# Layer 1 of the last two graphs in a two-layer graph kernel: gathered rows in one buffer, neighbour sums ordered ahead of the product with W, the graph's sum added on VectorE

## The chip, the cores and the metric

The kernel runs on one core of a Trainium2 chip. The metric is device time in microseconds of that core, the median of three runs. The kernel before takes 2736.29 us (2734.39 to 2737.78).

A core has five engines, each with its own queue of instructions: TensorE (PE, with its weight loads PEld), VectorE (DVE), ScalarE (ACT), GpSimd (POOL) and SyncE (SP). They wait for each other through semaphores. POOL issues the gathers and scatters (indirect DMAs); SP issues plain DMAs.

## What is computed

32 graphs share one adjacency matrix of 512 nodes; each node has 512 features, and about 1 in 128 entries of the matrix is 1, so a node has some four neighbours. Two layers follow each other, both with a residual:

```python
# layer 0: attention with 8 heads over the neighbours
h = relu(layernorm(x))
q, k, v = h @ Wq + bq, h @ Wk + bk, h @ Wv + bv
x = x + softmax(q k^T / 8 + (1 - adj) * -1e9) v @ Wo + bo
# layer 1: graph attention
h = relu(layernorm(x)) @ W
s1, s2 = h @ a1, h @ a2
e = leaky_relu(s1[i] + s2[j], 0.2) * adj
x = x + elu(softmax(e) h + beta * h)
```

In layer 1 the entries outside the adjacency are zero before the softmax, not minus infinity. So each row of the softmax is (sum over all nodes) plus a correction over the neighbours, with weight exp(e) - 1. The kernel therefore adds up the neighbours' rows with these weights, adds the graph's sum over all nodes, adds the node's own row times beta and the denominator, and only then multiplies by W, once.

## The kernel before, in words

**Tiles and stages.** A graph is cut into four tiles of 128 nodes. The edges of a tile are laid out as four groups of 128 edge slots. For each group one gather (an indirect DMA on POOL, L946) brings the neighbours' rows to the 128 partitions, and a matrix product with a 0/1 matrix (32 columns) sums the slots of each node into 32 rows of a PSUM tile. `stage_a` does norm, queries, keys and values of graph b; `stage_b` does the neighbour work of layer 0 for graph b and, LAG = 2 graphs behind, that of layer 1 for graph b - 2, out of the same gathered rows. After the last graph's layer 0 there is no layer 0 left to share with: for the last two graphs (30 and 31) `stage_b` runs with layer 1 alone and gathers 520-wide rows out of the tables `th0` and `th1`. A row holds the neighbour's s2 value at place 0 (HO) and its h row behind it.

**Layer 1 of one tile** (`edge_weights`, `layer1`), with the lines of the profile:

1. four gathers (L946), each 128 rows of 520 values, into two buffers of the ring `kv`, two rows to a buffer (a buffer holds 2 x 1552 values a partition, and there are five);
2. the edge weights: s1 + s2 (L1127, twice, one for each buffer), slope (L1131), exp on ACT (L1133), minus one and mask (L1134), spread over the 0/1 matrix into `wv` (L1140);
3. the neighbour sums on TensorE (L987, four instructions of the program, eight in the profile), and a product with one column for the denominators (L42, `pd<-one,wv`);
4. on DVE the denominators (L1162 to L1164) and the node's own row (L1170), for which ACT has made the relu of the norm (L756);
5. four transposes on TensorE (L737);
6. the graph's sum added while the transposed tile is moved from PSUM into `gT`: four ACT instructions, one for each 128 features, the sum as their bias (L1181);
7. the product with W on TensorE (L42, `pd<-w,gT`);
8. elu: two ACT instructions (L1190, L1191) and two on DVE (L1195, L1196), and a scatter of the tile to the output (L767 on POOL).

For the last two graphs the s1 values come by another way than for the others: they are transposed (L1100), copied by ACT (L1102), stored and read back by SP (L1103, L1108), and picked on DVE (L1112, L1113). The graph's sum comes from the column sums of h (L1081), copied by ACT (L1085), transposed and reduced (L1087).

**What sets the order.** All operations are given to a planner (`Plan`) with an engine, an estimated length, a due time (`key`) and the buffers that they read and write. The planner plays the program through with its estimates, gives out the buffers of each ring in the order of due times, and of the operations ready on an engine takes the one that is due first. What it writes out is a fixed order on every engine; the chip then runs that order with real waits. Due times count in steps of S = 20 for a tile: in layer 1, the sums at k = kb + S, the transposes and the graph's sum at k + 0.485 S, the product with W at k + 0.88 S, elu at k + 1.05 S and the store 0.15 S behind it; the edge weights at kb + 0.6 S.

Of the kernel before, what the change touches and what calls it, by code (L numbers as in the profile page):

```python
# [19 lines left out]
P = 128  # L20
# [19 lines left out]
def product(nc, out, lhsT, rhs, start=True, stop=True):  # L40

    nc.tensor.matmul(out, lhsT, rhs, start=start, stop=stop)  # L42
# [22 lines left out]
class Plan:  # L65
# [153 lines left out]
def kernel(  # L219
# [515 lines left out]
    def turned(p, src):  # L735
        for c in range(C):
            nc.tensor.transpose(p[:, ts(c, P)], src[:, ts(c, P)], ident)  # L737
# [196 lines left out]
    def stage_b(b):  # L934

        s = st[b] if b < B else None
        old = st[b - LAG] if b >= LAG else None
        if old is not None:
            old["dn"] = buf("dn", f"dn{b}")
        if s is not None:  # L940
            s["x1"], s["hx"] = [None] * T, [None] * T
            s["mv1"], s["s1"] = buf("mv1", f"mv1_{b}"), buf("s1", f"s1_{b}")
            s["rd"] = buf("rd", f"rd{b}")

        def gather(dst, tab, t, g):
            nc.gpsimd.indirect_dma_start(  # L946
                dst, None, tab.ap, bass.IndirectOffsetOnAxis(ap=idx[:, t, g : g + 1], axis=0),
                bounds_check=N + DUMMY - 1, oob_is_err=False,
            )

        for t in range(T):
            kb = base(T * b + t)
            slots = [buf("kv", f"kv{b}_{t}_{i}") for i in range(2)]
            held = [{n: buf(None, n) for n in ("K", "V", "H")} for _ in range(2)]
            of = {KO: "KVH", VO: "VH", HO: "H"}
            for g in range(NG):
                for tab, c0, c1 in st[b]["tab"]:
                    op("POOL", 1.3, kb - 0.85 * S + 0.1 * g, lambda sl=slots[g // 2], g=g, t=t, tab=tab, c0=c0, c1=c1: gather(
                        sl.ap[:, g % 2, c0:c1], tab, t, g),
                       r=[tab, C_["idx"]],  # L960
                       w=[(slots[g // 2], (g % 2, c0)), *((held[g // 2][n], (g % 2, "row")) for n in of[c0])],
                       dma=P * (c1 - c0) * 4)
            if s is not None:
                qs = [buf("qe", f"qe{b}_{t}_{i}") for i in range(2)]
                for q in qs:
                    q.q, q.s1 = buf(None, "q"), buf(None, "s1")
                for g in range(NG):
                    op("POOL", 1.3, kb - 0.84 * S + 0.1 * g, lambda q=qs[g // 2], g=g, t=t: nc.gpsimd.indirect_dma_start(  # L968
                        q.ap[:, g % 2, :], None, s["qtab"].ap,
                        bass.IndirectOffsetOnAxis(ap=qidx[:, t, g : g + 1], axis=0),  # L970
                        bounds_check=N, oob_is_err=False),
                       r=[s["qtab"], C_["qidx"]], w=[(x, g % 2) for x in (qs[g // 2], qs[g // 2].q, qs[g // 2].s1)],
                       dma=P * QW * 4)
            wvb = edge_weights(b - LAG, t, kb, slots, held, qs if s is not None else None) if old is not None else None
            pv = layer0(b, t, kb, slots, held, qs, old is not None) if s is not None else None
            if old is not None:
                layer1(b - LAG, t, kb, slots, held, wvb, pv)
                if t == T - 1:
                    op("DVE", 0.16, kb + 1.6 * S, lambda: nc.vector.tensor_tensor(
                        dmax, dmax, old["dn"].ap[:, 0:2, :], op=ALU.max), r=[old["dn"]], w=[C_["dmax"]])  # L980
        if s is not None:
            self_sums(b, base(T * b + 6))

    def edge_sums(out, lhs, slots, c0, n):

        for g in range(NG):
            nc.tensor.matmul(out(g), lhs(g), slots[g // 2].ap[:, g % 2, c0 : c0 + n], start=True, stop=True)  # L987
# [131 lines left out]
    def edge_weights(b, t, kb, slots, held, qs):  # L1119

        s = st[b]
        k1 = kb + 0.6 * S
        z, wvb = buf("z", f"z{b}_{t}"), buf("wv", f"wv{b}_{t}")
        for i in range(2):
            def add(i=i):
                s1 = s["s1e"].ap[:, t, 2 * i : 2 * i + 2] if qs is None else qs[i].ap[:, :, D]
                nc.vector.tensor_tensor(z.ap[:, 2 * i : 2 * i + 2], s1, slots[i].ap[:, :, HO], op=ALU.add)  # L1127
# [3 lines left out]
        op("DVE", 0.2, k1, lambda: nc.vector.scalar_tensor_tensor(  # L1131
            z.ap, z.ap, ALPHA, z.ap, op0=ALU.mult, op1=ALU.max), w=[z])
        op("ACT", 0.25, k1, lambda: nc.scalar.activation(z.ap, z.ap, AF.Exp), w=[z])  # L1133
        op("DVE", 0.2, k1, lambda: nc.vector.scalar_tensor_tensor(  # L1134
            z.ap, z.ap, -1.0, nzE[:, t, :], op0=ALU.add, op1=ALU.mult), r=[C_["nzE"]], w=[z])
        if b + LAG < B:
            for i in range(2):
                op("DVE", 0.1, k1, lambda i=i: nc.vector.tensor_copy(
                    slots[i].ap[:, :, HO], z.ap[:, 2 * i : 2 * i + 2]), r=[z, (slots[i], "use")], w=[(held[i]["H"], "z")])
        op("DVE", 0.35, k1, lambda: nc.vector.tensor_tensor(  # L1140
            wvb.ap.rearrange("p (g r) -> p g r", r=G), oh[:, ts(t, NG), :],
            z.ap.unsqueeze(2).to_broadcast([P, NG, G]), op=ALU.mult), r=[z, C_["OH"]], w=[wvb])
        return wvb

    def layer1(b, t, kb, slots, held, wvb, pv):
        s = st[b]
        px, g = buf("D", f"pg{b}_{t}"), buf("w", f"g{b}_{t}")
        o = op("PE", 1.02, kb + S, lambda: edge_sums(
            lambda i: px.ap[ts(i, G), :], lambda i: wvb.ap[:, ts(i, G)], slots, HO + 1, D),
               r=[*((x, "use") for x in slots), *((h["H"], "rows") for h in held), wvb], w=[px], form=4)  # L1150
        plan.reserve(o, g)
        k = kb + S
        x1, dn = s["x1"][t], s["dn"]
        op("ACT", 0.8, k, lambda: relu(g.ap, x1.ap, s["mv1"].ap, t), r=[x1, (s["mv1"], t)], w=[g])

        if pv is None:
            pd = buf("D", f"pn{b}_{t}")
            op("PE", 0.2, kb + S, lambda: product(nc, pd.ap[:, 0:1], wvb.ap, one32[:, 0:1]), r=[wvb], w=[pd])

        def den():  # L1160
            src, by = (pd.ap[:, 0:1], float(G)) if pv is None else (pv.ap[:, 1, 4 * VW : 4 * VW + 1], 1.0)
# [10 lines left out]
            )  # L1172

        op("DVE", 0.75, k, own, r=[px, (dn, t)], w=[g])
        pt, gT, py, y = buf("D", "pt"), buf("gT", f"gT{b}_{t}"), buf("D", "py"), buf("w", f"y{b}_{t}")
        oo = op("PE", 0.45, k + 0.485 * S, lambda: turned(pt.ap, g.ap), r=[g], w=[pt])
        plan.reserve(oo, gT)

        def add_all():
# [2 lines left out]
                    gT.ap[:, c, :], pt.ap[:, ts(c, P)], AF.Identity, bias=s["cs"].ap[:, c : c + 1]  # L1182
                )

        op("ACT", 1.5, k + 0.485 * S, add_all, r=[pt, s["cs"]], w=[gT])
        oo = op("PE", 3.43, k + 0.88 * S, lambda: dense(py.ap, gT.ap, w1), r=[gT, C_["w1"]], w=[py])
        plan.reserve(oo, y)

        def halves():
# [5 lines left out]
            nc.vector.scalar_tensor_tensor(y.ap, y.ap, 1.0, x1.ap, op0=ALU.min, op1=ALU.add)  # L1195
            nc.vector.tensor_tensor(y.ap, y.ap, py.ap, op=ALU.add)  # L1196
# [252 lines left out]
```

## Time and profile before

| | |
|---|---|
| median of three runs | 2736.29 us |
| the profiled execution's own time | 2723.47 us |
| its span | 2721.6 us |
| PE busy | 2648.3 us (97%) |
| DVE, ACT, POOL busy | 2049.9, 1934.4, 1831.2 us |
| DMA | 790 MB, 289 GB/s over the span |
| first product with W of graph 30 starts | 2649.42 us |
| last product with W of graph 31 starts | 2707.68 us |

The profile records one execution. The span runs from the first to the last instruction; times in it are counted from its start. A line of the timeline gives start, length, engine, line of the kernel, operation, output and input by the program's names (numbers of buffers left out), how many instructions are merged, and in brackets the engine's idle time before it and what ended that. `w` is a ring of row buffers, `pd` a ring of PSUM tiles; the matrix W has the program's name `w1`, shown as `w` in `pd<-w,gT`.

### The profile page before, as it was taken

Reading aid. Unit: us, or ns where it says so; the run is one execution under the profiler, and the core shown is the slowest. Engines: PE = TensorE matmul, PEld = TensorE weight load, DVE = VectorE, ACT = ScalarE, POOL = GpSimd, SP = SyncE. Lnnn points to the kernel's source line nnn. Section 1 sums busy time; section 2 is a strip of 40 time slices with the busy share of each in tenths; the row PEclk is TensorE's granted clock in tenths of the full one; section 3 lists DMA queues with packets and bytes.
Section 4 is the critical chain, followed back from the end, with each engine's and each line's share of the span. In section 5 each row is a group of like instructions: output and inputs, shape, how many; then the busy total and the mean of one; then the engine's idle time right before and its main releaser. Section 6 shows DMA issues by size and latency. Waiting matters only on the chain.

```text
span 2721.6 us, 39762 instructions
## 1 busy us (share of the span) xinstructions
PE 2648.3 (97%) x10220; PEld 1213.2 (45%) x10220; DVE 2049.9 (75%) x5200; ACT 1934.4 (71%) x6215; POOL 1831.2 (67%) x1710
## 2 busy tenths in 40 slices
PE   8999999999999999999999999999999999999886
PEld 4444444444444444444444444444444444444332
DVE  7768777777777777777777777777777777777663
ACT  1557777687877777777777777777777777777763
POOL 2776766666766766766766776676676676675763
PEclk9999999999999999999999999999999999999988
DMA  5988998888988988988988988988888888888863
GB/s 180 252 290 320 307 307 291 297 294 305 311 296 289 321 292 296 314 297 288 316 298 292 326 291 290 321 289 303 312 296 292 305 309 303 297 310 286 303 211 117
DMA packets 237457, 790.08 MB, mean 290 GB/s; under 512 B 34667, under 2 KB 34675, under 8 KB 237222
## 3 DMA queue, kind: packets, MB, share of 16 engines
q0 software_dynamic: 156736, 644.99, 70.3%
q1 hardware_dynamic: 80486, 142.48, 14.0%
q8 instruction: 83, 1.36, 0.2%
q14 instruction: 152, 1.25, 0.1%
HBM read 617.88 MB, written 169.46 MB: 289 GB/s over the span
## 4 chain that ended last, share of the span: by engine, by line
PE 88%; DMA 3%; issue 3%; DVE 2%; ACT 2%; POOL 2%; POOLq 0%; SPq 0%; DVEq 0%; ACTq 0%
PE pd L42 46%; PE pd L858 26%; PE pd L737 6%; PE pd L987 4%; PE px L987 4%; DMA qe<-qtab,qidx 1%; ACT kv L1014 1%; PE pd L918 1%; DMA kv<-tkv,idx 1%; PE pd L1081 1%; POOL kv L946 1%; POOL qe L968 0%; POOL x L762 0%; DMA x<-in_x_dram,perm 0%; DVE s L1003 0%
## 5 line engine op out<-in xcount | busy, mean ns | idle before, releaser
L1014 ACT ACTIVATE kv<-kv 128x64 f32<-128x64 f32 x4096 | 1011.8, 335 | 5.2
L968 POOL DMA_INDIRECT qe<-qtab,qidx x512 | 556.0, 1086 | 223.0 <-issue 114.0
L946 POOL DMA_INDIRECT kv<-tab,idx x480 | 508.2, 1059 | 164.6 <-issue 113.6
L42 PE MATMUL pd<-wo,oT 128*128 128x512 f32 x1032 | 468.6, 597 | 2.5 <-ACT oT L1051 2.4
L42 PE MATMUL pd<-w,gT 128*128 128x512 f32 x1024 | 466.1, 598 | 3.6 <-ACT gT L1181 3.6
L42 PE MATMUL pd<-wq,hT 128*128 128x512 f32 x1024 | 465.0, 597 | 2.2 <-ACT hT L782 2.2
L762 POOL DMA_INDIRECT x<-in_x_dram,perm x252 | 359.5, 1426 | 85.1 <-issue 50.3
L1000 DVE TENSOR_TENSOR qe<-qe,kv 128x1024 f32<-128x1024 f32 x256 | 312.1, 1220 | 44.4 <-DMA qe<-qtab,qidx 35.6
L1003 DVE TENSOR_REDUCE s<-qe 128x16 f32<-128x1024 f32 x256 | 310.5, 1214 | 0.1
L42 PEld LDWEIGHTS pd<-w,gT 128*128 128x128 f32 x1024 | 195.7, 192 | 249.5 <-issue 234.0
L42 PEld LDWEIGHTS pd<-wo,oT 128*128 128x128 f32 x1032 | 196.3, 192 | 245.0 <-issue 222.0
L42 PEld LDWEIGHTS pd<-wq,hT 128*128 128x128 f32 x1024 | 195.4, 192 | 245.6 <-issue 241.7
L749 POOL TENSOR_TENSOR mv<-mv,mhalf 128x1 f32<-128x1 f32 x256 | 171.4, 670 | 177.5 <-DVE mv L746 156.7
L767 POOL DMA_INDIRECT out_dram<-w,perm x128 | 157.3, 1229 | 149.8 <-DVE w L1196 105.7
L858 PE MATMUL pd<-wk,hT 128*128 128x512 f32 x496 | 239.7, 607 | 3.7 <-ACT hT L782 3.4
L858 PE MATMUL pd<-wt,S 128*128 128x512 f32 x496 | 238.5, 603 | 4.5 <-DVE k L866 4.1
L858 PE MATMUL pd<-wv,S 128*128 128x512 f32 x496 | 233.6, 593 | 3.1 <-DVE v L866 1.8
L1190 ACT ACTIVATE w<-pd,dn 128x512 f32<-128x512 f32 x128 | 87.6, 684 | 185.8 <-PE pd L42 185.5
L1061 DVE CUSTOM_DVE_ANT_0 w<-hx,wa_r 128x512 f32<-128x512 f32 x256 | 175.1, 684 | 11.3 <-ACT hx L756 10.5
L1053 DVE TENSOR_TENSOR x<-pd,x 128x512 f32<-128x512 f32 x128 | 87.9, 687 | 121.8 <-PE pd L42 110.1
L744 DVE BATCH_NORM_STATS2 st<-x 128x6 f32<-128x512 f32 x256 | 176.3, 689 | 3.8 <-DMA x<-in_x_dram 1.0
L737 PE MATMUL pd<-ident,w 128*128 128x128 f32 x1152 | 154.3, 276 | 21.7 <-DVE w L1038 11.2
(204 smaller groups left out, 3504.7 us busy)
## 6 DMA issues: line engine op xcount, KB each, us to landing
qtab<-q SPq DMA_DIRECT2D x124, 258.0 KB
tab<-hx SPq DMA_DIRECT2D x120, 260.0 KB
tab<-v SPq DMA_DIRECT2D x120, 260.0 KB
tab<-k SPq DMA_DIRECT2D x120, 256.0 KB
qe<-qtab,qidx POOLq DMA_INDIRECT x512, 7.8
kv<-tab,idx POOLq DMA_INDIRECT x480, 8.0
x<-in_x_dram,perm POOLq DMA_INDIRECT x252, 8.0
th<-hx SPq DMA_DIRECT2D x8, 260.0 KB
```

The costliest lines, as they stand in the source:

```text
L42: nc.tensor.matmul(out, lhsT, rhs, start=start, stop=stop)
L737: nc.tensor.transpose(p[:, ts(c, P)], src[:, ts(c, P)], ident)
L744: nc.vector.bn_stats(s6.ap, src.ap)
L762: nc.gpsimd.indirect_dma_start(dst, None, rows, bass.IndirectOffsetOnAxis(ap=perm[:, t : t + 1], axis=0), **lim)
L858: nc.tensor.matmul(p.ap, lhs()[:, c, :], rhs[:, c, :], start=first and c == 0, stop=c == K2 - 1, skip_group_check=True)
L946: nc.gpsimd.indirect_dma_start(dst, None, tab.ap, bass.IndirectOffsetOnAxis(ap=idx[:, t, g : g + 1], axis=0), bounds_check=N + DUMMY - 1, ...
L968: op("POOL", 1.3, kb - 0.84 * S + 0.1 * g, lambda q=qs[g // 2], g=g, t=t: nc.gpsimd.indirect_dma_start(q.ap[:, g % 2, :], None, s["qtab"]. ...
L987: nc.tensor.matmul(out(g), lhs(g), slots[g // 2].ap[:, g % 2, c0 : c0 + n], start=True, stop=True)
L1000: nc.vector.tensor_tensor(qe.ap[:, :, 0:D], qe.ap[:, :, 0:D], sl.ap[:, :, KO : KO + D], op=ALU.mult)
L1003: nc.vector.tensor_reduce(sb.ap, qe.ap[:, :, 0:D].rearrange("p n (h f) -> p n h f", f=HD), axis=AX.X, op=ALU.add)
L1014: nc.scalar.activation(p[:, h, 0:HD], p[:, h, 0:HD], AF.Copy, scale=p[:, h, HD : HD + 1])
L1061: nc.vector.tensor_tensor_reduce(scr.ap, hx.ap[:, 1 : D + 1], row, 1.0, 0.0, op0=ALU.mult, op1=ALU.add, accum_out=dst)
```

## The change

Four things change, all for graphs with b + LAG >= B, which are the last two:

- A tile's four gathered rows of 520 values lie behind each other in one buffer of the ring `kv`, in place of two rows in each of two buffers. `row` and `weights_of` give the addresses.
- Due times: the sums at kb + 0.5 S in place of kb + S; transposes and graph's sum at kb + 0.6 S; the product with W at kb + 1.7 S, elu at kb + 1.75 S; the edge weights at kb + 0.2 S in place of kb + 0.6 S. In the built order this puts the denominators and the sums of tile n + 1 between the transposes of tile n and its product with W.
- The graph's sum is added by one DVE instruction over 128 x 512, the sum broadcast along each run of 128, in place of four ACT instructions.
- The transposed tile alternates between the buffers `gT` and `oT`.

Since the planner lays out everything anew, other instructions of the last stretch move too. On POOL, the four gathers of a tile now stand together. The gathers of graph 30's tile 0 now have the last `qe` gathers of layer 0 between the third and the fourth, where all but the first two stood behind them; the square root for the norm (L749), the output store and the fetch of `x` come after these four gathers. On DVE, L751 (which waits for L749) comes after the next L1127, L1138 and L1140, and the pick of graph 31's s1 (L1112, L1113) comes after the graph's sum of graph 30's tile 3, where it came after graph 30's tile 2. On ACT, one L1009 comes ahead of two relus.

```diff
+    GL, ZL = 0.5, 0.2
...
-            slots = [buf("kv", f"kv{b}_{t}_{i}") for i in range(2)]
+            slots = [buf("kv", f"kv{b}_{t}_{i}") for i in range(2 if s is not None else 1)]
+            slots += slots[len(slots) - 1 :] * (2 - len(slots))
...
+    def row(slots, g, c0, n):
+
+        if slots[0] is slots[1]:
+            return slots[0].ap.rearrange("p a b -> p (a b)")[:, g * HW_ + c0 - HO : g * HW_ + c0 - HO + n]
+        return slots[g // 2].ap[:, g % 2, c0 : c0 + n]
+
+    def weights_of(slots, i):
+
+        if slots[0] is slots[1]:
+            flat = slots[0].ap.rearrange("p a b -> p (a b)")[:, 0 : NG * HW_]
+            return flat.rearrange("p (g c) -> p g c", g=NG)[:, 2 * i : 2 * i + 2, 0]
+        return slots[i].ap[:, :, HO]
...
-            nc.tensor.matmul(out(g), lhs(g), slots[g // 2].ap[:, g % 2, c0 : c0 + n], start=True, stop=True)
+            nc.tensor.matmul(out(g), lhs(g), row(slots, g, c0, n), start=True, stop=True)
...
-        k1 = kb + 0.6 * S
+        k1 = kb + (0.6 if b + LAG < B else ZL) * S
...
-        o = op("PE", 1.02, kb + S, lambda: edge_sums(
+        last = b + LAG >= B
+        k = kb + (GL if last else 1.0) * S
+        kt, kw, ke = (0.6 - GL, 1.7 - GL, 1.75 - GL) if last else (0.485, 0.88, 1.05)
+        o = op("PE", 1.02, k, lambda: edge_sums(
...
-        pt, gT, py, y = buf("D", "pt"), buf("gT", f"gT{b}_{t}"), buf("D", "py"), buf("w", f"y{b}_{t}")
-        oo = op("PE", 0.45, k + 0.485 * S, lambda: turned(pt.ap, g.ap), r=[g], w=[pt])
+        pt, gT, py, y = buf("D", "pt"), buf("oT" if last and t % 2 else "gT", f"gT{b}_{t}"), buf("D", "py"), buf("w", f"y{b}_{t}")
+        oo = op("PE", 0.45, k + kt * S, lambda: turned(pt.ap, g.ap), r=[g], w=[pt])
...
-        op("ACT", 1.5, k + 0.485 * S, add_all, r=[pt, s["cs"]], w=[gT])
-        oo = op("PE", 3.43, k + 0.88 * S, lambda: dense(py.ap, gT.ap, w1), r=[gT, C_["w1"]], w=[py])
+        def add_at_once():
+            nc.vector.tensor_tensor(
+                gT.ap, pt.ap.rearrange("p (c q) -> p c q", c=C), s["cs"].ap.unsqueeze(2).to_broadcast([P, C, P]), op=ALU.add)
+
+        if last:
+            op("DVE", 0.72, k + kt * S, add_at_once, r=[pt, s["cs"]], w=[gT])
+        else:
+            op("ACT", 1.5, k + kt * S, add_all, r=[pt, s["cs"]], w=[gT])
+        oo = op("PE", 3.43, k + kw * S, lambda: dense(py.ap, gT.ap, w1), r=[gT, C_["w1"]], w=[py])
...
-        op("ACT", 1.36, k + 1.05 * S, halves, r=[(dn, t)], w=[py, y])
-        op("DVE", 1.45, k + 1.05 * S, elu, r=[py, x1], w=[y])
-        op("POOL", 1.3, k + 1.2 * S, lambda: keep(y.ap, b, t), r=[y, C_["perm"]], dma=P * D * 4)
+        op("ACT", 1.36, k + ke * S, halves, r=[(dn, t)], w=[py, y])
+        op("DVE", 1.45, k + ke * S, elu, r=[py, x1], w=[y])
+        op("POOL", 1.3, k + (ke + 0.15) * S, lambda: keep(y.ap, b, t), r=[y, C_["perm"]], dma=P * D * 4)
```

More of the change, by code (lines that the diff above doesn't have):

```diff
@@ L957, in stage_b @@
                 for tab, c0, c1 in st[b]["tab"]:
-                    op("POOL", 1.3, kb - 0.85 * S + 0.1 * g, lambda sl=slots[g // 2], g=g, t=t, tab=tab, c0=c0, c1=c1: gather(
-                        sl.ap[:, g % 2, c0:c1], tab, t, g),
+                    op("POOL", 1.3, kb - 0.85 * S + 0.1 * g, lambda slots=slots, g=g, t=t, tab=tab, c0=c0, c1=c1: gather(
+                        row(slots, g, c0, c1 - c0), tab, t, g),
                        r=[tab, C_["idx"]],
-                       w=[(slots[g // 2], (g % 2, c0)), *((held[g // 2][n], (g % 2, "row")) for n in of[c0])],
+                       w=[(slots[g // 2], (g, c0)), *((held[g // 2][n], (g % 2, "row")) for n in of[c0])],
                        dma=P * (c1 - c0) * 4)
@@ L1126, in add @@
                 s1 = s["s1e"].ap[:, t, 2 * i : 2 * i + 2] if qs is None else qs[i].ap[:, :, D]
-                nc.vector.tensor_tensor(z.ap[:, 2 * i : 2 * i + 2], s1, slots[i].ap[:, :, HO], op=ALU.add)
+                nc.vector.tensor_tensor(z.ap[:, 2 * i : 2 * i + 2], s1, weights_of(slots, i), op=ALU.add)
             op("DVE", 0.2, k1, add, r=[*([s["s1e"]] if qs is None else [(qs[i], "use"), qs[i].s1]),
@@ L1138, in edge_weights @@
                 op("DVE", 0.1, k1, lambda i=i: nc.vector.tensor_copy(
-                    slots[i].ap[:, :, HO], z.ap[:, 2 * i : 2 * i + 2]), r=[z, (slots[i], "use")], w=[(held[i]["H"], "z")])
+                    weights_of(slots, i), z.ap[:, 2 * i : 2 * i + 2]), r=[z, (slots[i], "use")], w=[(held[i]["H"], "z")])
         op("DVE", 0.35, k1, lambda: nc.vector.tensor_tensor(
@@ L1151, in layer1 @@
         plan.reserve(o, g)
-        k = kb + S
         x1, dn = s["x1"][t], s["dn"]
@@ L1157, in layer1 @@
             pd = buf("D", f"pn{b}_{t}")
-            op("PE", 0.2, kb + S, lambda: product(nc, pd.ap[:, 0:1], wvb.ap, one32[:, 0:1]), r=[wvb], w=[pd])
+            op("PE", 0.2, k, lambda: product(nc, pd.ap[:, 0:1], wvb.ap, one32[:, 0:1]), r=[wvb], w=[pd])
         def den():
```

## The prediction

> **What bounds the kernel now.** I read the busy shares first (TensorE 97% of the span), then the stretches by engine, then TensorE's timeline at the end, then who waits for whom there. Up to about 2500 us it hardly rests, and the change does not reach there. In the built orders the first instructions that differ are due at about 2613 us (POOL) and 2616 us (DVE); everything ahead of them is the same. So only the last 108 us count. The stretch that holds the eight tiles of the last two graphs' layer 1, and the one after it (columns: length, then busy us and count of PE, PEld, DVE, ACT, POOL, then clock, DMA share, GB/s):
>
> ```profile
> 2649.40:2711.40 62.00, 49.36 (x175) 19.94 (x175) 25.59 (x86) 23.89 (x60) 29.38 (x29) 0.92 0.46 137
> 2711.40:2721.60 10.20, 0.10 (x2) 0.00 (x0) 1.52 (x3) 1.24 (x2) 0.98 (x1) 0.73 0.09 32
> ```
>
> No engine is full: a chain through three engines sets the pace. One tile's turn on TensorE (start, length, what, idle time before it and its releaser):
>
> ```profile
> 2670.73 0.38 PE L42 MATMUL pd<-one,wv 128*128 128x1 f32 x2
> 2673.72 0.66 PE L737 MATMUL pd<-ident,w 128*128 128x128 f32 x4 [2.61 <-DVE w L1170]
> 2674.90 5.40 PE L42 MATMUL pd<-w,gT 128*128 128x512 f32 x8 [0.52 <-ACT gT L1181]
> 2680.22 1.07 PE L987 MATMUL pd<-kv,wv 128*32 128x512 f32 x8
> 2681.22 0.38 PE L42 MATMUL pd<-one,wv 128*128 128x1 f32 x2
> 2682.32 0.66 PE L737 MATMUL pd<-ident,w 128*128 128x128 f32 x4 [0.72 <-DVE w L1170]
> 2683.49 3.70 PE L42 MATMUL pd<-w,gT 128*128 128x512 f32 x8 [0.52 <-ACT gT L1181]
> ```
>
> Sum, own row (L1170), transposes, graph's sum (L1181), W's product: TensorE rests twice a tile, and after a rest of 2.61 us the product takes 5.40 instead of 3.60. The eight products start at 2649.42, 2656.41, 2664.41, 2674.90, then 2683.49, 2692.29, 2700.79, 2707.68: 8.3 us apart. Once two tiles stand back to back, which shows what TensorE alone needs:
>
> ```profile
> 2655.14 0.66 PE L737 MATMUL pd<-ident,w 128*128 128x128 f32 x4
> 2655.64 0.28 PE L42 MATMUL pd<-one,wv 128*128 128x1 f32 x2
> 2655.92 0.66 PE L737 MATMUL pd<-ident,w 128*128 128x128 f32 x4
> 2656.41 3.60 PE L42 MATMUL pd<-w,gT 128*128 128x512 f32 x8
> 2659.95 1.06 PE L987 MATMUL pd<-kv,wv 128*32 128x512 f32 x8
> ```
>
> Start to start: transposes 0.50, column of denominators 0.28, product 3.54; the sum 0.98 (2655.92 to 2659.95 holds 0.49 and 3.54; 2669.74 to 2670.73 is a sum): 5.3 us a tile, against 8.3.
>
> [...] the trace has DVE idle at L751 with other work behind it (below). [...] L1196, which reads PSUM, takes 688. [...] the trace has 3.6 from issue to landing, and that is used.
>
> **The change part by part.**
>
> *Graph's sum on DVE.* Removes four ACT instructions (1.14 us together, the first 0.37 releasing TensorE, which starts 0.52 after the transposes); adds one DVE add that no row shows in this form; nearest row L1196, 0.69, and 0.05 at each end: TensorE could start 0.8 after the transposes. That 0.3 is hidden in seven tiles by the next tile's sum and denominators (0.98+0.28), and bare in the last. Bounds 0.6 to 1.2.
>
> *Sums of tile n+1 ahead.* TensorE's order becomes transposes n, denominators n+1, sum n+1, product n. The own row of n+1 (0.75) then runs under product n (3.54), and both rests go: 5.3 + 0.1 = 5.4 us a tile, at full clock. For this the weights wv of n+1 must exist before product n, so gathers and the z operations move forward. Four gathers into one buffer of five let whole tiles be fetched ahead; reading them at other addresses, and every second transposed tile in oT (unused once layer 0 is over), costs nothing: same shapes, same counts.
>
> *POOL's queue, early.* Two more gathers of tile 0 now stand before the last layer-0 tile's work. Before, POOL's timeline:
>
> ```profile
> 2613.69 0.99 POOL L968 DMA_INDIRECT qe<-qtab,qidx  x1 [0.30 <-DVE z L1131]
> 2614.99 1.00 POOL L968 DMA_INDIRECT qe<-qtab,qidx  x1 [0.30 <-issue]
> 2616.01 0.59 POOL L749 TENSOR_TENSOR mv<-mv,mhalf 128x1 f32<-128x1 f32 x1
> 2618.88 1.23 POOL L767 DMA_INDIRECT out_dram<-w,perm  x1 [2.29 <-DVE w L1196]
> ```
>
> and DVE's:
>
> ```profile
> 2616.63 0.16 DVE L751 SCALAR_TENSOR_TENSOR mv<-mv 128x1 f32<-128x1 f32 x1 [0.74 <-POOL mv L749]
> ```
>
> Each gather costs 1.3 (1.0 busy, 0.3 issue). L749 slips 2.6, to 2618.65, and DVE stands at L751 until 2619.3 (2.6 late), with L1195, L1196 and the output store, L1061, L1038 queued behind. L1038 moves from 2619.73 to 2622.0, its transposes from 2620.47 to 2622.7. But ACT was the late one there: its 16 L1014 end at 2623.4 and oT's copy follows. Now hx's relu waits for L751, so the 16 run 2620.7 to 2624.6, oT at 2625.1, Wo's product at 2625.2 instead of 2623.94: 1.3 late. For the next tile kv4's gathers (issued 2629.9 and 2631.2, landed about 2635.2 with 3.5 to 4 us each) hold DVE's z add ahead of L1195: another 0.5. So the last Wo product starts at 2639.15 instead of 2637.39: 1.8 late (bounds 0 and 4). It takes 5.23 as before; then denominators 0.35, sum of tile 0 0.98, graph 29's product 3.54, 0.3, transposes 0.5, sum of tile 1 0.98, 0.3: tile 0's product starts at 2651.3, 1.9 late.
>
> *Graph 30.* To tile 1's product: 5.3 + column sums 0.98 + s1's transpose 0.23 = 6.5. To tile 2's: 5.3 + csr's transposes 0.5 = 5.8. To tile 3's there is a new wait. Graph 31's s1 values (L1112, L1113) stand on DVE behind tile 3's graph add, which waits for tile 3's transposes, and TensorE wants wv of graph 31's tile 0 before tile 3's product. After the transposes: add 0.8, L1112 and L1113 1.4, elu of tile 2 1.4, four z adds 0.35, slope 0.25, exp 0.45, mask 0.2, wv 0.3 = 5.1 us of rest. Before, that work lay under products. The clock falls, so denominators and sum take 2.4. Distance: 3.54 + 0.55 + 5.1 + 2.4 = 11.6. Bounds of the rest: 3 (s1 pick first through) and 8.
>
> *Graph 31.* First distance 6.8 (cold product 5.0, then 1.8), then 5.4, 5.4, and 4.9 (3.54 + 0.5 + bare add 0.8, no next sum). Gathers: graph 31's start when hx's last rows are stored. L1061 is at 2649 instead of 2649.87; POOL then issues 16 gathers and 3 stores from 2653.5, at 1.3 each: the last lands at 2653.5 + 15x1.3 + 4.0 + 3.7 = 2680.7, and DVE asks for it at about 2683. Hidden by 2 us.
>
> *Sum.* 2651.3 + 6.5 + 5.8 + 11.6 + 6.8 + 5.4 + 5.4 + 4.9 = 2697.7 for the last product, against 2707.68: 10.0 earlier. From there on nothing changes (3.7 product, L1190, L1195, L1196, store, 10.2 to the end). Span 2721.6 - 10.0 = 2711.6. The profiled execution took 2723.5 while the median is 2736.3; I apply the difference to the median: 2726.3. Note where it comes from: graph 30's last product starts 0.5 *later* than before (2675.2 instead of 2674.9), and all of the gain is in graph 31.
>
> **The rivals.**
>
> *The boundary rest does not appear, nor the early delay* (pow and pick meet slack): for it, POOL had 2.29 us of rest at 2616; against it, the order on DVE. Saves 5.1 + 1.9 + some 1.5 of cold clock more, 18.5 in all: 2717.8.
>
> *Gathers become the bound.* For it: POOL is now in one line from 2653.5 to 2678, 2 us ahead of need; against it: DMA share 0.46. The last landing is 61.2 + 15p with p us per gather, so from p = 1.45 on each 0.1 costs 1.5 us. At p = 1.8 the gain is 4.8: within 0.2%, about 2731.5.
>
> *Slower.* The same chain at p = 2.6, with the landing 17 us past need: -10 + 17 = 7 us slower, 2743. It loses from p = 2.1, and is measurably slower from 2.5. The longest single gathers here took 2.03 + 0.3 while wide layer-0 rows moved; the tail's mean is 1.04 + 0.3. Unlikely.
>
> *The change doesn't do what it says*: if DVE's add costs more than the hiding sums (above 1.3), each tile loses the excess: at 1.7, 7 x 0.4 = 3 us, 2729, still faster.
>
> **How the numbers follow.** Measurement of this kernel can tell about 0.2%, 5.5 us. Likeliest, 10 us less, its own range 6 to 14 (early delay 0 to 4, boundary rest 3 to 8): 0.63, the dear add included, and 0.03 of it under 5.5. No rest: 0.18. Gathers bound: 0.14. Slower by over 0.2%: 0.05. Faster 0.60 + 0.18 + 0.03 of the third = 0.81; same 0.14; slower 0.05. The range leaves out the slower end, the last us of the gathers' case and the lower tip of the first rival (runs spread by 1.7 us): 2716.5 to 2733.5.
>
> **What would show it.** Right: products of graph 31 5 to 6 us apart, at 3.6 each; one rest of about 5 us at the graphs' boundary, released by wv; DVE waiting about 2.6 at L751; at the first graph's end no gain. Wrong: rests before sums released by gathers; transposes waiting for L1170; products at 5.4 throughout; a change before 2610 us.

## The result, and the profile after

The changed kernel takes 2725.46 us (median of 14 runs, 2719.87 to 2730.99) against 2733.02 us for the kernel before (14 runs, 2727.55 to 2737.78). The ratio is 0.9972, 95% interval 0.9963 to 0.9981: 7.6 us faster (5.2 to 10.1). The prediction was 2726.3 us.

| | before | after |
|---|---|---|
| the profiled execution's own time | 2723.47 us | 2723.72 us |
| its span | 2721.6 us | 2721.9 us |
| PE busy | 2648.3 us | 2645.6 us |
| DVE, ACT, POOL busy | 2049.9, 1934.4, 1831.2 us | 2054.0, 1939.6, 1824.3 us |
| the eight W products start over | 58.3 us (2649.42 to 2707.68) | 51.7 us (2656.27 to 2708.01) |

The two spans are equal, yet the tail is shorter: the work ahead of the change took longer in the execution that was profiled after (2552.5 us to the begin of the tail, against 2546.3 before). So I compare traces by their **tail**: from the start of the seventh-last product with Wo, which lies at 2546 us of before and ahead of everything that differs, to the end of the span. It is 175.3 us before and 169.4 us after, 5.9 less. There is one trace of the kernel before, so how far its tail varies from execution to execution is not known.

The lines of after that answer to those shown of before. First the stretch of the eight products by engine (length, then busy us and count of PE, PEld, DVE, ACT, POOL, then clock, DMA share, GB/s):

```profile
2656.20:2711.70 55.50, 43.30 (x167) 18.95 (x167) 27.89 (x85) 14.88 (x27) 24.47 (x24) 0.91 0.38 115
```

The stretch is 6.5 us shorter (62.00 before), ScalarE's busy time fell from 23.89 to 14.88 us, VectorE's rose from 25.59 to 27.89. Now TensorE's timeline at the boundary between the two graphs and after it (start, length, what, idle time before it and its releaser):

```profile
2665.73 1.04 PE L738 MATMUL pd<-ident,w 128*128 128x128 f32 x8
...
2666.81 1.07 PE L1002 MATMUL pd<-kv,wv 128*32 128x512 f32 x8
2669.78 3.70 PE L42 MATMUL pd<-w,gT 128*128 128x512 f32 x8 [1.90 <-issue]
2675.55 0.66 PE L738 MATMUL pd<-ident,w 128*128 128x128 f32 x4 [2.06 <-DVE w L1188]
2683.66 0.58 PE L42 MATMUL pd<-one,wv 128*128 128x1 f32 x2 [7.45 <-DVE wv L1155]
...
2686.03 5.20 PE L42 MATMUL pd<-w,oT 128*128 128x512 f32 x8
2691.07 0.60 PE L738 MATMUL pd<-ident,w 128*128 128x128 f32 x4
2691.51 0.28 PE L42 MATMUL pd<-one,wv 128*128 128x1 f32 x2
2691.72 1.07 PE L1002 MATMUL pd<-kv,wv 128*32 128x512 f32 x8
2692.72 3.70 PE L42 MATMUL pd<-w,gT 128*128 128x512 f32 x8
```

(L738, L1002, L1188, L1155 are L737, L987, L1170, L1140 of before.) The last four lines are a tile of the second graph as forecast: transposes, denominators, sum and product without a rest, the product at 3.70. The products of that graph follow each other by 6.7, 5.2, 5.2 and 4.9 us; those of the first graph by 6.0, 7.5 and 16.3. So the gain is there, and a boundary of 16.3 us, where I had 11.6, takes a good part of it. VectorE at the same place, and ahead of it one line of 43 us earlier:

```profile
2624.31 0.16 DVE L752 SCALAR_TENSOR_TENSOR mv<-mv 128x1 f32<-128x1 f32 x1 [1.98 <-POOL mv L750]
...
2667.53 0.17 DVE L1102 TENSOR_REDUCE cs<-pd 128x4 f32<-128x16 f32 x1 [4.07 <-PE pd L42]
2669.04 0.69 DVE L1204 TENSOR_TENSOR gT<-pd,cs 128x512 f32<-128x512 f32 x1 [1.34 <-PE pd L1002]
2674.74 0.75 DVE L1188 SCALAR_TENSOR_TENSOR w<-w,dn,pd 128x512 f32<-128x512 f32 x1 [3.25 <-PE pd L42]
2678.97 0.69 DVE L1204 TENSOR_TENSOR oT<-pd,cs 128x512 f32<-128x512 f32 x1 [3.38 <-remote]
```

The first is the wait for the norm's square root that the prediction spoke of (L751 of before). Each of the other four reads what TensorE made and starts well after TensorE's own lines say that it was done (the profile calls the releaser of the last one `remote`): the transposes for the add at 2669.04 ended at 2666.8, those for the add at 2678.97 at 2676.2. The order on VectorE that I had put the rest down to (add, pick, elu, weights) is there as well, from 2678.97 to 2683.66, where the rest of 7.45 us ends. ScalarE waits longest of all there, with the elu of tile 2, whose product ended at 2673.5 by TensorE's own line:

```profile
2677.53 0.69 ACT L1215 ACTIVATE w<-pd,dn 128x512 f32<-128x512 f32 x1 [9.13 <-PE pd L738]
```

Which of the two, waits or order, costs what was the first question.

### The profile page after: what moved, and what is told of

It reads as the page before. It is cut to its first block, busy times and chain, and to the rows that moved or that the text cites. A ratio compares the mean times of both kernels' runs of the same rounds, so it can differ in the third digit from the quotient of the medians.

```text
span 2721.9 us, 39740 instructions
## 1 busy us (share of the span) xinstructions
PE 2645.6 (97%) x10220; PEld 1213.4 (45%) x10220; DVE 2054.0 (75%) x5208; ACT 1939.6 (71%) x6183; POOL 1824.3 (67%) x1710
## 3 DMA queue, kind: packets, MB, share of 16 engines
q14 instruction: 152, 1.25, 0.1%
## 4 chain that ended last, share of the span: by engine, by line
PE 91%; DVE 3%; issue 2%; DMA 2%; ACT 1%; POOL 1%; another core or an unknown queue 0%; POOLq 0%; SPq 0%; DVEq 0%; ACTq 0%
PE pd L42 48%; PE pd L859 27%; PE pd L738 6%; PE pd L1002 4%; PE px L1002 4%; PE pd L919 1%; PE pd L1096 1%; DMA qe<-qtab,qidx 1%; ACT kv L1029 0%; POOL kv L947 0%; DMA x<-in_x_dram,perm 0%; DMA kv<-tab,idx 0%; DVE s L1018 0%; DVE st L745 0%; POOL qe L970 0%
## 5 line engine op out<-in xcount | busy, mean ns | idle before, releaser
L42 PE MATMUL pd<-w,gT 128*128 128x512 f32 x992 | 446.4, 593 | 1.9 <-issue 1.9
L42 PEld LDWEIGHTS pd<-w,gT 128*128 128x128 f32 x992 | 188.1, 190 | 240.2 <-issue 230.6
L750 POOL TENSOR_TENSOR mv<-mv,mhalf 128x1 f32<-128x1 f32 x256 | 169.7, 664 | 169.0 <-DVE mv L747 146.9
L1215 ACT ACTIVATE w<-pd,dn 128x512 f32<-128x512 f32 x128 | 88.0, 688 | 177.0 <-PE pd L42 161.3
L738 PE MATMUL pd<-ident,w 128*128 128x128 f32 x1152 | 154.5, 276 | 23.2 <-DVE w L1053 20.0
```

## The experiments

The runs came in three groups of four, in the order of the table. In each, the kernel before ran beside them on the same chip, and the ratios are against it: 2742.45 us in the first group, 2732.87 in the second, 2726.80 in the third. "Less" is the time under the kernel before, worked out from ratio and interval; "tail" is that of each kernel's own trace, to be held against 175.3. The changed kernel itself gained 7.6, 12.6 and 5.5 us in three measurements, so gains of different groups can be several us apart with no change in the kernel; the two traces of the early pick have tails 1.1 us apart.

| run | ratio (95% interval) | less, us | tail, us |
|---|---|---|---|
| changed kernel | 0.9972 (0.9963 to 0.9981) | 7.6 | 169.4 |
| again | 0.9954 (0.9939 to 0.9970) | 12.6 | 169.4 |
| pick_early | 0.9960 (0.9944 to 0.9976) | 11.0 | 164.6 |
| weights_early | 0.9940 (0.9925 to 0.9955) | 16.5 | 165.1 |
| gathers_later | 0.9948 (0.9930 to 0.9965) | 14.3 | 169.7 |
| again_2 | 0.9980 (0.9970 to 0.9990) | 5.5 | 169.5 |
| pick_early_2 | 0.9971 (0.9961 to 0.9981) | 7.9 | 163.5 |
| order_alone | 0.9957 (0.9944 to 0.9971) | 11.8 | 164.7 |
| sum_on_act | 0.9967 (0.9955 to 0.9979) | 9.0 | 167.5 |
| order_early | 0.9944 (0.9931 to 0.9956) | 15.3 | 159.9 |
| two_buffers | 0.9953 (0.9940 to 0.9965) | 12.8 | 161.5 |
| twice | 1.0018 (1.0011 to 1.0026) | -4.9 | 182.1 |
| dve_alone | 1.0037 (1.0025 to 1.0049) | -10.1 | 184.5 |

### The changed kernel once more

No edit.

> The changed kernel once more, for a second profile. Its first profile has 16.25 us between the products of tiles 2 and 3 of the first of the two graphs (forecast 11.6), and three waits of 1.3 to 3.4 us on VectorE just ahead of that which no data seems to call for. Theory A (order on VectorE: graph add, pick of s1, elu, weights): the rest ahead of the first sum of the last graph is 5 us, the three waits are an accident of that one execution, and the distance is now 11 to 13 us. Theory B (the waits belong to the kernel): 16 us again. Time 7 to 8 us under the kernel before under both.

Theory B by the profile: the distances are 6.0, 7.6, 16.3, 6.3, 5.2, 5.2, 4.9, and VectorE's waits agree within 0.05 us; ScalarE's longest is 9.18. The waits are no accident of one execution. The gain, 12.6 us (8.2 to 16.7), is more than the expected 7 to 8, with a wide interval.

### The pick of s1 ahead of tile 3's graph sum

```diff
-           r=[row], w=[s1b], dma=P * N * 4)
+           r=[row], w=[s1b], dma=2048 if b + 1 == B else P * N * 4)
```

The planner then takes the read-back for shorter and places the pick earlier; no transfer is changed.

> The pick of s1 for the last graph (two instructions on VectorE, 1.4 us) ahead of the graph's sum of tile 3 instead of behind it, nothing else moved. Theory A: the pick then runs under a product, the rest at the boundary is 1.4 us shorter: 1 to 2 us faster than the changed kernel, 8.5 to 9.5 us under the kernel before. Theory B (TensorE's own completion is what is late, not VectorE's line): no difference, within 0.5 us of the changed kernel.

By the times theory B, by the trace neither. The trace's tail became 4.8 us shorter, more than three times what the pick lasts: the distances are 6.0, 8.3, 9.1, 6.6, 5.2, 5.2, 4.9, and the waits at L1188 and at the last add are gone. But the time is that of the changed kernel beside it (2731.07 against 2730.71 us): tail and time do not go together here.

### The pick and the weights of the last graph's first tile ahead

```diff
     todo = plan.order()
+    first = [o for o in todo if o in early]
+    todo = [o for o in todo if o not in early]
+    at = todo.index(target[0])
+    todo[at:at] = first
```

`early` holds the pick of graph 31 and the six operations of its tile 0's edge weights, `target` the first half of tile 2's elu (L1215) of graph 30.

> The pick of s1 and the whole chain of the edge weights of the last graph's tile 0 (sum, slope, exp, mask, spread) ahead of the graph's sum of tile 3 on VectorE, the exp ahead of the elu of tile 2 on ScalarE. Theory A: the rest of 5 us or more ahead of the first sum of the last graph goes almost wholly, and the cold clock behind it too (sum 1.9 and product 5.2 in place of 1.07 and 3.6): 6 to 9 us faster than the changed kernel, some 15 us under the kernel before. Rival: the s1 values come back from memory too late (written out and read back by SyncE), the rest only moves ahead of tile 2's or 3's graph add: 0 to 2 us.

Tail 4.3 us shorter, time 2727.56 against 2730.71 us for the changed kernel: in the right direction, less than the 6 to 9 expected, and the two intervals overlap. In the trace the boundary is still 12.9 us, with the late completions in it. Left open here; the same move is tried again below.

### Two gathers behind the norm's square root

```diff
     todo = plan.order()
+    todo = [o for o in todo if o not in later]
+    at = todo.index(dict(roots)["b31_1"]) + 1
+    todo[at:at] = later
```

`later` holds the third and fourth gather of graph 30's tile 0; `roots` names the square roots.

> The third and fourth gather of the first of the two graphs' tile 0 behind the square root for the norm on GpSimd, as in the kernel before; all else as in the changed kernel. My prediction put 1.8 us of delay on these two gathers (VectorE idle 2.6 us at L751 of before, TensorE 1.8 us later from there on). If it is right: 1 to 2 us faster than the changed kernel, and no rest of VectorE there. Rival, that ScalarE was the late one there and the delay is swallowed: within 0.5 us.

The rival. VectorE's wait for that square root, 1.98 us in the changed kernel (L752 above), is down to what it was before (0.74):

```profile
2635.39 0.16 DVE L754 SCALAR_TENSOR_TENSOR mv<-mv 128x1 f32<-128x1 f32 x1 [0.67 <-POOL mv L751]
```

But the first product with W starts 104.1 us after the tail's begin, as in the changed kernel (103.8 and 104.1), and the tail is 169.7. The longer wait was there, and cost nothing.

### The changed kernel and the early pick on another chip

> The changed kernel a third time, beside the next run on the same chip. In both profiles so far TensorE's completions come out evenly paced from the end of tile 1's product on (1.43 us for the eight records of four transposes, 2.86 for the sixteen of a product, 0.18 us a record whatever the work), which makes the distance from tile 2 to tile 3 16.3 us in place of some 11. Theory C (that pacing is a matter of the recorded execution and not of the plain ones): 16.3 us again in the profile, and the plain executions no slower than those of the next run by more than 1.5 us. Theory D (it is there in all executions): 16.3 us in the profile, and 5 to 7 us slower than the next run in the plain executions too.

> The pick of s1 ahead of tile 3's graph sum once more; its first profile was 6.5 us shorter from the last Wo product to the end than that of the changed kernel, its plain executions were not. Theory C: 0 to 1.5 us faster than the changed kernel beside it. Theory D: 5 to 7 us faster.

In the changed kernel's trace the first distance is 6.0 again; the next two are 5.5 and 18.5 in place of 7.6 and 16.3, with the same sum: the late completions begin one product later, and the tail is 169.5 once more. The early pick gives 6.0, 6.4, 12.9 and a tail of 163.5. The times are 2726.22 and 2723.13 us: 3.1 us apart, between what theory C allows (1.5) and what D asks for (5 to 7). With 0.4 us the other way in the first group, the two kernels are far closer in time than their traces. But against the kernel before, the changed one gained 5.5 us here (2.7 to 8.2), close to what its trace says (5.9). So neither theory holds for all of it.

### Due times alone, and the sum back on ScalarE

order_alone, against the changed kernel:

```diff
-            slots = [buf("kv", f"kv{b}_{t}_{i}") for i in range(2 if s is not None else 1)]
+            slots = [buf("kv", f"kv{b}_{t}_{i}") for i in range(2)]
...
-        if last:
+        if False:
             op("DVE", 0.72, k + kt * S, add_at_once, r=[pt, s["cs"]], w=[gT])
```

sum_on_act has only the second of these edits. Both keep the fourth part of the change, the turn-taking of `gT` and `oT`; no run took that away, so "due times alone" below means the due times with it.

> The due times alone: sums of tile n + 1 ahead of the product of tile n, but two gathered rows to a buffer as before and the graph's sum on ScalarE. My theory (the order is what gains; the one buffer is needed to fetch whole tiles ahead; the add on VectorE is worth little): most of the gain, with TensorE resting before sums where gathers come late: 3 to 8 us under the kernel before. Rival (the two buffers a tile leave only five halves for tiles ahead, so the sums wait for gathers at each tile): no gain, 0 to 3 us slower than before.

> The changed kernel with the graph's sum back on ScalarE (four instructions a tile, 1.14 us); the due times and the one buffer stay. ScalarE then has the four adds, the two of elu, relu and exp, 3.6 us of a 5.4 us tile. My theory: the adds end 1.2 us after the transposes and are hidden by the sum and denominators (1.26 us): within 1 us of the changed kernel, or faster by up to 3 us, since the pick of s1 then comes earlier on VectorE. Rival (the adds queue behind the elu of the tile before on ScalarE): 1.4 us a tile lost, 8 to 11 us slower than the changed kernel.

The due times alone gain 11.8 us (7.9 to 15.3), more than the 3 to 8 expected: neither the one buffer nor the add on VectorE is needed for the gain. With the sum on ScalarE and the one buffer it is 9.0, 1.8 us faster than the changed kernel beside it, as my theory allowed; ScalarE's adds do not queue to a loss. In order_alone the distances are 8.1, 5.6, 11.1, 8.4, 5.3, 5.3, 5.3: the second graph runs at 5.3 us a tile with ScalarE's four adds too, 0.1 more than with VectorE's one, and the last product shows the longer add (a rest of 1.18 against 0.78 us):

```profile
2681.03 0.59 PE L42 MATMUL pd<-one,wv 128*128 128x1 f32 x2 [4.62 <-DVE z L1149]
...
2697.11 3.70 PE L42 MATMUL pd<-w,oT 128*128 128x512 f32 x8
...
2702.43 3.70 PE L42 MATMUL pd<-w,gT 128*128 128x512 f32 x8
...
2707.74 3.70 PE L42 MATMUL pd<-w,oT 128*128 128x512 f32 x8 [1.18 <-ACT oT L1199]
```

The first of these lines is the boundary rest, here 4.62 us.

### Two buffers with the add on VectorE

Only the first of the two edits above.

> The changed kernel with two buffers to a tile as before (due times and VectorE's add stay). The due times alone gave 11.8 us, with the one buffer 9, with buffer and add 5.5 to 7.6. If the buffer is what costs (gathers of whole tiles in one line on GpSimd, earlier, ahead of the norm's square root): 9 to 11 us under the kernel before. If the add on VectorE is what costs: 6 to 8 us. In the profile the first shows as no evenly paced completions, the second as the 16 us boundary again.

12.8 us, more than I gave it, and no late completions: 8.3, 5.2, 12.0, 5.9, 5.2, 5.2, 4.9. By the expectation's wording the buffer is what costs. But the run below says that this would be too quick.

### Each gather of the last graph twice

```diff
+            spare = buf("kv", f"spare{b}_{t}") if b == B + 1 else None
...
+                    if spare is not None:
+                        op("POOL", 1.3, kb - 0.85 * S + 0.1 * g + 0.05, lambda spare=spare, ...: gather(
+                            row([spare, spare], g, c0, c1 - c0), tab, t, g),
+                           r=[tab, C_["idx"]], w=[(spare, (g, c0))], dma=P * (c1 - c0) * 4)
```

> The changed kernel with each of the sixteen gathers of the last graph done twice, the second time into a buffer that nobody reads; output as before. GpSimd has 16 x 1.3 = 21 us more to issue. My prediction had the last landing 2 us ahead of its need and each 0.1 us more per gather worth 1.5 us, so 1.3 us more per gather: 17 us slower than the changed kernel (minus what the boundary turned out longer, 5 us: 12 to 17). Rival (gathers are far from the bound): less than 3 us slower.

4.9 us slower than the kernel before (3.0 to 7.1), so some 12 us slower than the changed kernel by its gain of 7.6, and 12.7 by the tails: as expected. GpSimd issues one transfer after the other from 2676 to 2707, 1.3 us apiece, and the weights wait for landings. TensorE's timeline:

```profile
2665.44 1.07 PE L1007 MATMUL pd<-kv,wv 128*32 128x512 f32 x8
2666.44 3.70 PE L42 MATMUL pd<-w,gT 128*128 128x512 f32 x8
2669.97 0.60 PE L738 MATMUL pd<-ident,w 128*128 128x128 f32 x4
2675.17 0.59 PE L42 MATMUL pd<-one,wv 128*128 128x1 f32 x2 [4.59 <-DVE wv L1160]
...
2677.55 5.05 PE L42 MATMUL pd<-w,oT 128*128 128x512 f32 x8
...
2686.24 0.38 PE L42 MATMUL pd<-one,wv 128*128 128x1 f32 x2 [3.20 <-DVE wv L1160]
```

The rest of 3.20 us ahead of the second tile's denominators is one that the changed kernel doesn't have. It is not a wait for a landing: the planner, with more gathers to place, put that tile's weights behind an add and an elu on VectorE (2683.08 to 2685.08). The waits for landings themselves last 0.5 to 2.0 us, five of them in the second graph. So the loss is in part one of order, and the run does not price the gathers cleanly. This trace says something else as well. On TensorE, and on VectorE up to the weights of the second graph's first tile, its instructions come in the order of the changed kernel, with the one buffer and the add on VectorE; what differs is on GpSimd. Yet nothing is late: the distances are 6.0, 5.5, 11.1, and tile 2's product follows its sum at once. The rest ahead of the second graph is 4.59 us, and VectorE's timeline shows what it is made of (and, in its last line, the longest wait for a landing):

```profile
2670.61 0.69 DVE L1209 TENSOR_TENSOR oT<-pd,cs 128x512 f32<-128x512 f32 x1 [1.69 <-PE pd L738]
2671.22 0.68 DVE L1132 TENSOR_TENSOR q<-OH,q 128x512 f32<-128x512 f32 x1
2671.94 0.69 DVE L1133 TENSOR_REDUCE s1e<-q 128x16 f32<-128x512 f32 x1
2672.54 0.68 DVE L1225 SCALAR_TENSOR_TENSOR w<-w,x 128x512 f32<-128x512 f32 x1
2673.32 0.69 DVE L1226 TENSOR_TENSOR w<-w,pd 128x512 f32<-128x512 f32 x1
...
2674.82 0.29 DVE L1160 TENSOR_TENSOR wv<-OH,z 128x128 f32<-128x128 f32 x1
...
2702.37 0.16 DVE L1147 TENSOR_TENSOR z<-s1e,kv 128x2 f32<-128x2 f32 x1 [2.03 <-DMA kv<-th,idx]
```

Add, pick, elu, weights, each as soon as the one before is done: the forecast's boundary, without the late completions. So the order on TensorE and VectorE does not by itself bring these about; GpSimd's queue, the chip and the recording differ as well.

### The add on VectorE alone

The kernel before with `add_at_once` for the last two graphs, at the old due times.

> The kernel before with VectorE's one add in place of ScalarE's four in the last two graphs, due times and buffers as before; the orders on the other engines stay. Bare, TensorE starts 0.8 us after the transposes in place of 0.52: 8 x 0.3 = 2.4 us slower, if VectorE is free when the transposes end. The elu of the tile before stands ahead of the add in some tiles: then up to 1.4 us more a tile. So 2 to 6 us slower than the kernel before; a rival says the same time within 1 us.

10.1 us slower (6.8 to 13.4), beyond the upper end. One tile on TensorE, and VectorE there:

```profile
2689.73 0.66 PE L737 MATMUL pd<-ident,w 128*128 128x128 f32 x4 [0.71 <-DVE w L1170]
2692.10 5.29 PE L42 MATMUL pd<-w,gT 128*128 128x512 f32 x8 [1.71 <-DVE gT L1186]
```

```profile
2689.97 0.68 DVE L1202 SCALAR_TENSOR_TENSOR w<-w,x 128x512 f32<-128x512 f32 x1
2690.76 0.69 DVE L1203 TENSOR_TENSOR w<-w,pd 128x512 f32<-128x512 f32 x1
2691.36 0.69 DVE L1186 TENSOR_TENSOR gT<-pd,cs 128x512 f32<-128x512 f32 x1
```

The transposes end at 2690.4, but elu of the tile before (1.4 us) stands ahead of the add. TensorE rests 1.71 us in six tiles and 0.93 and 1.34 in the others, where it was 0.52 with ScalarE's first add: 8.4 us more in all, and the tail is 9.1 longer.

### Due times alone, with the weights of the last graph's first tile ahead

order_alone with the edit of weights_early.

> The due times alone (two buffers, the graph's sum on ScalarE), and with them the pick and the edge weights of the last graph's tile 0 ahead of the elu of tile 2 on VectorE, their exp ahead of it on ScalarE. In the due times alone the boundary takes 11.1 us from tile 2's product to tile 3's and then 8.4 with a cold product (5.9), with the weights released at 2681 by an exp that stood behind the late adds of tile 3. If that line is what costs: weights some 3.7 us earlier and a warm clock, 5 to 7 us faster than the due times alone, 16 to 18 us under the kernel before. Rival (the slow completions of TensorE just move to another wait): 0 to 2 us.

15.3 us less (12.0 to 18.8), and the shortest tail of all; weights_early's 16.5 us in another group can't be told from it. Against the due times alone, on another chip, it is 3.5 us more in time and 4.8 in the tail, where 5 to 7 were expected. The boundary:

```profile
2662.33 3.70 PE L42 MATMUL pd<-w,gT 128*128 128x512 f32 x8
2665.87 0.60 PE L739 MATMUL pd<-ident,w 128*128 128x128 f32 x4
2666.97 0.38 PE L42 MATMUL pd<-one,wv 128*128 128x1 f32 x2 [0.50 <-DVE wv L1161]
...
2668.28 3.70 PE L42 MATMUL pd<-w,oT 128*128 128x512 f32 x8
```

0.50 us of rest in place of 4.62, the product at 3.70, and 5.95 us from product to product where it was 11.1. The next three distances are 7.0, 7.0 and 6.3, where they were 8.4, 5.3 and 5.3: with the boundary rest gone, VectorE waits for gathers ahead of each tile's weights (1.2 to 1.6 us a time), and the sums wait behind it.

## Why the prediction came out as it did

The number was right: 2726.3 forecast, 2725.46 measured, and 10 us of gain forecast against 7.6 (5.2 to 10.1). Its steps, one by one:

**Where the change begins.** Nothing speaks against it. The product with Wo at 2609 us of before, the last ahead of the first difference, lies 62.9 us into the tail; in four traces with the changed early order (the three of the changed kernel and twice) it lies 61.9 to 63.3 us in. The three traces of the changed kernel have the same tail within 0.1 us.

**The early delay.** Its cause is wrong, and its size is not shown. VectorE stood 1.98 us at the norm, where 2.6 was forecast; in the same four traces the last Wo product came 0.7 to 2.6 us later against the tail's begin, where 1.8 was forecast, and the first W product 0.6 to 1.0 later, where it was 1.9. But gathers_later took the two gathers away from in front of the square root, and nothing came earlier. And dve_alone, whose order up to the last Wo product is that of before on every engine, has that product 1.0 us later than before as well. A delay of this size comes without any change ahead of it.

**The distances.** In the trace without late completions (twice) 6.0, 5.5 and 11.1 us where 6.5, 5.8 and 11.6 were forecast; in the changed kernel's own second graph 6.1 to 6.7, 5.2, 5.2 and 4.9, where 6.8, 5.4, 5.4 and 4.9 were. At the boundary itself the changed kernel has 16.3 and 18.5 in place of 11.6. That the clock would fall in that rest was an estimate of mine; in the changed kernel's first trace it is granted at 0.50 from about 2679 to 2689 us, where denominators and sum take 2.37 us (2.4 forecast) and the product 5.20 (5.0 forecast). The bare add in the last tile costs a rest of 0.78 us; 0.8 was forecast. From the last product's start to the end it is 13.9 us in both kernels.

**The boundary rest.** Right where the late completions are absent: 4.59 us in twice, forecast 5.1, bounds 3 to 8, by the very chain (add, pick, elu, weights). It is 4.62 in order_alone and 5.47 in two_buffers; in the changed kernel's own first trace it is 7.45. order_early takes it out and has the shortest tail. The rival in which it does not appear fell.

**No gain at the first graph's end.** Nearly: without late completions its last product comes 2.1 us earlier than before (126.6 us into the tail against 128.6), where 0.5 later was forecast. In the changed kernel's own traces it comes 4.9 to 5.6 us later than before. The gain lies in the second graph, as forecast: from that product to the last one of all 21.3 to 22.0 us, where it was 32.8 and 22.5 was forecast.

**The sum.** Put together from measured terms (103.9 to the first product, 6.0, 5.5, 11.1, then 6.3, 5.2, 5.2, 4.9, and 13.9) the tail would be 162.0 us, 13 us less than before; my terms, each a little long, gave 10. The changed kernel's traces show 5.9 instead, for the late completions take 7 us at the boundary, and its times show 7.6, 12.6 and 5.5. So the forecast stands between what its mechanism is worth and what the chip gave, and part of its closeness is luck: a wait that I did not foresee ate what I had priced too low. Besides, the 10 us were taken off 2736.3, while the kernel before ran at 2733.0 beside the changed one; part of the agreement of 2726.3 with 2725.46 is that too.

**One buffer.** Wrong, where it stands as what the new order rests on: four gathers into one buffer were to "let whole tiles be fetched ahead". With two buffers the same due times gain 12.8 us; without late completions both reach the first graph's last product within 0.2 us of each other (126.4 and 126.6). Reading the four rows at other addresses did not lengthen the sums: at a granted clock of 1.00 they take 1.05 to 1.08 us in after (L1002) and 1.06 to 1.07 in before (L987).

**The sum on VectorE.** Right that it is hidden in the new order; it takes 0.69 us (L1204), as the nearest row of before had it (L1196, 0.69). The price without cover was mis-sized: I had 0.3 us a tile, dve_alone shows 1.2 in six of eight, since elu stands ahead of the add on the same queue.

**The gathers as the bound.** In the changed kernel they are not the bound at 1.3 us a gather: in the second graph's last three tiles TensorE rests ahead of no sum. A gather took 3.6 us from issue to landing in the tail of before, the figure that the prediction used. With the issue doubled (2.6) the forecast was 7 us slower than before; it was 4.9 (3.0 to 7.1), and 6.8 by the trace. The size fits, but part of it comes from VectorE's new order in that run, so the price per gather is not shown.

## What to carry to other kernels

When work of the next tile is moved ahead of a product, look at the first tile of the next batch: what makes its inputs may still stand where it was, and the rest that the move takes away everywhere comes back there once (4.59 us in twice, 4.62 in order_alone). Price an operation that moves to another engine by what stands ahead of it in that queue, not by its own length: the same 0.69 us add is hidden in one order (in after no rest stands ahead of the products at 2692.72, 2697.90 and 2703.09) and costs 10.1 us in the other (dve_alone). And take a change of several parts apart: here the due times alone ran 3.5 us faster than the whole beside them on the same chip (2722.71 against 2726.22).

## What was not expected of the hardware

**Late completions.** In all three traces of the changed kernel TensorE's completions come evenly paced for some 13 us at the boundary (2666.05 to 2678.94 in the first), counted by the semaphores that it raises: 1.43 us for the eight records of four transposes, 2.86 for the sixteen of a product, less than the product itself takes (3.70). VectorE and ScalarE, which wait for them, stand for up to 3.4 us and 9.1 us, of which 4 us lie behind the product's end by TensorE's line. Meanwhile TensorE went on: its transposes at 2675.55 start before the completion of the product ahead of them is seen at 2677.5. The profile models the ends of TensorE's instructions, so whether the work itself or only the word of it was late is not shown. The cause is open. All traces with such a stretch, and those of the same two groups with little of it, hold some 28,600 to 29,800 semaphore events (29,585 beside 39,740 instructions in the changed kernel's first); the five without any (the kernel before and the third group) some 41,200 to 41,400 (41,216 beside 39,762 in before). The third group also ran on another chip than the other two. So every trace with the stretch has the lower count of events; whether the recording holds TensorE up is not shown. The times don't settle it. Each timed execution of the changed kernel has a span and a granted clock on record, so none is known to have run unrecorded. The changed kernel's profiled executions (2723.72, 2729.07 and 2726.77 us) are no slower than the medians of their runs (2725.46, 2730.71 and 2726.22), so the paced stretch, some 7 us, is likely in the others too. Its gains fit the paced tail (5.9) better than an even one (13) in two of three measurements (7.6 and 5.5 us), and the other way in the third (12.6). The changed kernel was not run in the third group, so whether its time there would be 5 us better is not known.

**A cold product after short rests.** In dve_alone no rest of TensorE is longer than 1.9 us in the stretch of the eight products; still five of them take 5.29 us or more, four after rests of 0.7 and 1.7 us in the same tile. The granted clock is 0.68 or 0.69 in those four, and 1.00 in the three products of 3.70, as in before (0.68 or 0.69 in its products of 5.30 and 5.40, 1.00 in those of 3.60 and 3.70). One of these three follows the same two rests:

```profile
2681.64 0.66 PE L737 MATMUL pd<-ident,w 128*128 128x128 f32 x4 [0.72 <-DVE w L1170]
2684.01 3.70 PE L42 MATMUL pd<-w,gT 128*128 128x512 f32 x8 [1.71 <-DVE gT L1186]
```

In before, too, the third product took 5.40 us with no rest in its tile longer than 1.25:

```profile
2662.27 0.38 PE L42 MATMUL pd<-one,wv 128*128 128x1 f32 x2 [1.25 <-DVE wv L1140]
2663.24 0.66 PE L737 MATMUL pd<-ident,w 128*128 128x128 f32 x4 [0.58 <-DVE w L1170]
2664.41 5.40 PE L42 MATMUL pd<-w,gT 128*128 128x512 f32 x8 [0.52 <-ACT gT L1181]
```

So one long rest is not needed for a slow product, and the prediction's pair (5.40 after a rest of 2.61 us, 3.70 after 0.72) is not a rule of this kernel. What sets the clock in these tiles stays open.
